# Statistics in smaller pieces between two additions, and two blocks that stay in fast memory, in a four-layer scan kernel

## The chip, the cores and the metric

The kernel runs on one core of a Trainium2 chip. The metric is device time in microseconds (us) of one execution. Several executions of the same kernel are run, and their median is given. One further execution is taken by the hardware profiler; all profile views come from that one. Engines are named as in the profile: PE (TensorE matmul), PEld (its weight load), DVE (VectorE), ACT (ScalarE), POOL (GpSimd), SP (SyncE, which issues DMAs).

## The reference

The input is 4 x 48 x 256 x 256 numbers in float32. Four layers follow each other, each of the form x + layer(group norm of x). Layers 0 and 1 are an attention over channels and a gated convolution; the change does not touch them. Layers 2 and 3 are scans in four directions, with a five-tap convolution at each step:

```python
def step(w, b):
    def f(carry, inp):
        nxt = inp + _conv1d(carry, w, b)
        return (nxt, nxt)
    return f
# down over rows, up over rows (same weights), right over columns, left over columns
x = x + _L2_conv_ref(_gn(x), ...)   # scans' layer 0 below
x = x + _L3_conv_ref(_gn(x), ...)   # scans' layer 1 below
```

The group norm ahead of layer 3 needs mean and variance of the result of layer 2, over groups of three channels and all pixels.

## The kernel before

The four images are worked on as two pairs of two. For each pair the function `chain` writes one chain of steps: in each of two layers 256 steps down, 256 up, 256 right, 256 left. Of the two layers, `layer == 0` is the reference's layer 2 and `layer == 1` its layer 3. In a step (line 1067 and the lines after it) each image of the pair, `b`, has three matmuls into a PSUM bank `ps`, and then one addition on DVE that makes the new `carry` from `ps` and the step's input (line 1071 or 1075). The next step of the same image starts from this `carry`. The two images of a pair alternate, so that PE multiplies for one while DVE adds for the other.

The first pair's chain starts some 990 steps ahead of the second's (`LEAD`). So the first pair does nearly all of its first layer alone, then both chains share the engines step by step, and the second pair does nearly all of its last layer alone. The instructions of an engine run in one order that the framework's scheduler fixes when the kernel is built, from the order of writing and from priorities; `keep_in_program_order` holds an instruction in its written place. `look` (line 1044) is a tiny addition on DVE that reads one number of a buffer written three steps earlier; it is held in this way.

Columns are treated in NK = 16 blocks of CB = 16 steps. A buffer, called a slot, holds one block of one pair: 96 partitions x 4096 numbers, 1536 KB. Each pair has a ring of five slots, and `slot(name)` or `take(pair, name)` gives the next. In the right scan `lines` collects a block's results with an addition of the bias on ACT (line 1291), and at the end of the block it is stored in DRAM as `R` (line 1305). `pre` are columns copied on POOL (line 1264). The left scan goes through the blocks backwards. At the first step of block n it issues, on SP, the load of `lines` of block n - 1 from `R` (line 1327) and that of `stage`, the layer's input to which the result is added (line 1328). For each step POOL adds the new carry to a column of `stage` (line 1339), and at the end of the block `stage` is stored (line 1359). In the last layer of the second pair (`direct`) POOL writes instead into two buffers `done` (line 1343), taken from the first pair's ring, one for each image and holding two blocks; they are stored straight into the output by `write` (line 1371). By then the first pair is finished; its slots were last used by `to_rows`, which brings the first pair's result into rows with copies on POOL and ACT (lines 1450 and 1452) while the second pair runs its last layer. The list `times` says at which steps its pieces are written.

In `layer == 0` the left scan also takes the statistics for the next group norm. For each block, `late` gets 8 pieces: for each image four times `bn_stats` over 512 numbers (line 1380). One is taken out at the end of each of the following steps. After the last block the remaining ones are written, then for each image one `bn_aggr` over all 64 pieces, which gives `mv` (line 1400), then the group norm's two short pieces, each with a matmul (lines 88 to 99).

Of the kernel before, what the change touches and what calls it, by code (L numbers as in the profile page):

```python
# [9 lines left out]
F32 = mybir.dt.float32  # L10
# [8 lines left out]
NP = 2  # L19
P = 96  # L20
# [5 lines left out]
NK = W // (2 * KC)  # L26
# [938 lines left out]
def scans(ctx, tc, xs, out, wts, biases, dram, k, coefs, lead, spare):  # L965
# [13 lines left out]
    nc = tc.nc  # L979
# [42 lines left out]
    def chain(pair):  # L1022
# [23 lines left out]
        def slot(name):  # L1046
            return take(pair, f"{name}{pair}")
# [55 lines left out]
        def layer_of(layer, first):  # L1103
# [33 lines left out]
            for n in range(NT):  # L1137
                ahead_ = None
                for r in range(RT):
# [12 lines left out]
                    def keep(new, b):  # L1152
                        nc.scalar.activation(inp[:, b], blocks(new[:, b]), AF.Identity, bias=bias[:, 0:1])  # L1153
# [111 lines left out]
                fetched[g] = t  # L1265

            kept.clear()
            column = columns[0]
            for w in range(1, far):
                fetch(column, 0, w)  # L1270
            for n in range(NK):
                ahead_ = None
                for w in range(CB):
                    if w == 0 and n == 0:
                        ahead_ = columns[1]
                    elif w == 0 and n + 1 < NK:
                        ahead_ = slot("col")
                        nc.sync.dma_start(by_batch(ahead_), block_of(U, n + 1))
                    if w == 0 and n + 1 == NK:
                        stage = slot("stage")  # L1280
                        nc.sync.dma_start(by_batch(stage), block_of(x, n))
                    if w == 0:
                        lines = slot("lines")
                    if w + far < CB:
                        fetch(column, n, w + far)
                    elif ahead_ is not None:
                        fetch(ahead_, n + 1, w + far - CB)
                    line = lines_view(lines)[:, w]

                    def keep(new, b):  # L1290
                        nc.scalar.activation(line[:, b], new[:, b], AF.Identity, bias=bias[:, 2:3])  # L1291

                    if n == 0 and w == 0:

                        nc.vector.tensor_scalar(  # L1295
                            advance(), cols_view(column)[:, :, 0, :, 0], bias[:, 1:2], None, ALU.subtract
                        )
                        keep(inner(), slice(0, 2))
                    else:
                        step(layer, 1, fetched.pop(n * CB + w), keep)  # L1300
                    if n + 1 < NK or w + 1 < CB:
                        look(line[:, 1, 0:1], fetched[n * CB + w + 1][:, 1, 0:1])
                    yield
                if ahead_ is not None:
                    nc.sync.dma_start(Rt[n], lines)
                    column = ahead_


            late = []
            if layer == 0:  # L1310
                stats = [wp.tile([P, NK * 4, 6], F32, tag=f"st{pair}{b}", name="st") for b in range(2)]
            following = None
            kept.clear()

# [5 lines left out]
            for n in reversed(range(NK)):  # L1320
# [2 lines left out]
                    done = [take(0, "done") for _ in range(2)]  # L1323
                for w in reversed(range(CB)):
                    if w == CB - 1 and n > 0:
                        ahead_ = slot("lines"), slot("stage")
                        nc.sync.dma_start(ahead_[0], Rt[n - 1])
                        nc.sync.dma_start(by_batch(ahead_[1]), block_of(x, n - 1))
                    if layer == 0 and n == 0 and w == CB // 2:
                        following = [slot("dn"), slot("dn")]  # L1330
                        for r in range(2):
                            load_rows(1, 0, r, following[r], 1, NK)
                    line = lines_view(lines)[:, w]
                    to = cols_view(stage)[:, :, w % 2, :, w // 2]

                    def keep(new, b):
                        if not direct:
                            if b.stop == 2:
                                nc.gpsimd.tensor_add(to, to, new)  # L1339
                            return  # L1340
                        for i in range(b.start, b.stop):
                            place = done[i].rearrange("p (h w) -> p h w", w=2 * CB)[:, :, n % 2 * CB + w]
                            nc.gpsimd.tensor_add(place, to[:, i], new[:, i])  # L1343

                    if n == NK - 1 and w == CB - 1:
                        keep(inner(), slice(0, 2))
                    else:
                        step(layer, 2, line, keep)
                    if direct:
                        look(done[1].rearrange("p (h w) -> p h w", w=2 * CB)[:, 0, n % 2 * CB + w : n % 2 * CB + w + 1])  # L1350
                    else:
                        look(to[:, 1, 0:1])
                    if late:
                        late.pop(0)()
                    if writes and w % 8 == 4:
                        writes.pop(0)()
                    yield
# [19 lines left out]
                if layer == 0:  # L1377

                    def stat(b, c, n=n, v=by_batch(stage)):
                        nc.vector.bn_stats(stats[b][:, n * 4 + c, :], v[:, b, c * 512 : (c + 1) * 512])  # L1380

                    late += [lambda b=b, c=c, f=stat: f(b, c) for b in range(2) for c in range(4)]
                    if n == 0:
                        for r in range(2):
                            for q in range(2):
                                nc.sync.dma_start(
                                    rows_view(following[r])[q * C : (q + 1) * C, :, 0].rearrange("c b h w -> c b (h w)"),
                                    cols_view(stage)[r * C : (r + 1) * C, :, q, :NH, :].rearrange("c b h w -> c b (h w)"),
                                )
# [4 lines left out]
            if layer == 0:  # L1394

                ends = []
                for b in range(2):
                    mv = work.tile([P, 2], F32, tag=f"mv{pair}{b}", name="mv")
                    late.append(
                        lambda b=b, mv=mv: nc.vector.bn_aggr(mv, stats[b].rearrange("p a b -> p (a b)"))  # L1400
                    )
                    ends.append(k.group_norm_pieces(work, p_small, mv, "mean6", coefs[3][2 * pair + b], f"{pair}{b}"))
                for piece in late:
                    piece()
                    yield
                for i in range(2):
                    for both in ends:
                        both[i]()
                    yield
                yield following  # L1410
# [58 lines left out]

    engines = [nc.gpsimd] * 4  # L1470
    pieces = to_rows(0, engines)
    times = [20 + 26 * i for i in range(16)] + [530 + 24 * i for i in range(8)]
    for i, _ in enumerate(chains[1]):
        if i == times[16]:
            engines[3] = nc.scalar
# [127 lines left out]
```

## Time and profile before

| what | value |
|---|---|
| median of 3 runs | 8981.94 us (8981.17 to 8982.99) |
| the profiled execution | 8983.88 us; its span 8982.1 us |
| mean granted clock of PE | 0.983 |
| PE busy | 8646.3 us, 96% of the span |
| DVE busy | 4167.5 us, 46% |
| ACT busy | 3479.8 us, 39% |
| POOL busy | 1948.9 us, 22% |
| matmuls of the scans (line 1067) | 48960 records, 5423.7 us busy, 12 for each step of a pair |
| statistics of the left scan (line 1380) | 256, 172.3 us busy |
| aggregates after the left scan (line 1400) | 4, 7.4 us busy |

A line of the group view reads: line, engine, operation, tiles out<-in, shapes, count | busy time and mean ns of one | idle time of the engine before them, and what ended it. A line of the windows view reads: window, its length, busy time (and instructions) of PE, PEld, DVE, ACT and POOL, then the mean granted clock of PE, the mean busy share of the 16 DMA engines, and GB/s. A line of the timeline reads: start, length, engine, source line, operation, tiles, shapes, count, and in brackets the engine's idle time and what ended it. In the chain of waits the first column is the start and the second the length of a piece, and each piece released the next. Times count from the start of the span.

In the profiled execution the first statistic of the first pair begins at 4537.0 us, the last one of the second pair at 7495.2 us. The second pair's last left scan has its first addition at 8594.7 and the last at 8949.2 us.

### The profile page before, as it was taken

The page shows a single profiled execution, that of the slowest core. Times are in us where ns is not written, and L with a number is a line of the kernel's source. Part 1 is how long each engine was busy: PE and PEld are TensorE (multiplying, and loading weights), DVE is VectorE, ACT ScalarE, POOL GpSimd, SP SyncE. Part 2 cuts the span into 40 slices and gives each one's busy share as a digit, 9 for nine tenths or more (in the row PEclk, how much of TensorE's full clock was granted, in tenths as well). Part 3 has the DMA queues.
Part 4 walks back from the last instruction along what each step waited for, and adds up shares of the span by engine and source line. Part 5 has one row for each costly group of instructions (what it writes and reads, how often), then busy time and mean ns, then how long its engine had stood idle before and what let it go on. Part 6 is the DMA issues. An engine that isn't in the chain of part 4 may idle for free. (4 is left out here: it accounts for less than half of the span.)

```text
span 8982.1 us, 162711 instructions
## 1 busy us (share of the span) xinstructions
PE 8646.3 (96%) x62920; PEld 7223.1 (80%) x62920; DVE 4167.5 (46%) x15625; ACT 3479.8 (39%) x7023; POOL 1948.9 (22%) x3100
## 2 busy tenths in 40 slices
PE   6999999999999978999999999999999999999998
PEld 4777777533333335999999999999999999999998
DVE  3231110234555555445666444445666555444653
ACT  0010101123433455766601776666663003665610
POOL 0000000001111111001454000001445664101575
PEclk9999999999999988999999999999999999999998
DMA  7654323367888876765577664556656887867789
GB/s 152 132 125 94 74 61 77 82 140 160 173 181 182 182 165 162 168 138 143 155 190 190 152 139 120 141 135 141 169 146 175 216 220 181 198 172 191 210 176 183
DMA packets 1180233, 1390.64 MB, mean 155 GB/s; under 512 B 263184, under 2 KB 1107216, under 8 KB 1118784
## 3 DMA queue, kind: packets, MB, share of 16 engines
q1 hardware_dynamic: 1179360, 1379.90, 65.7%
q8 instruction: 493, 8.08, 0.4%
q14 instruction: 284, 2.33, 0.1%
q0 software_dynamic: 96, 0.33, 0.0%
HBM read 811.21 MB, written 509.61 MB: 147 GB/s over the span
## 5 line engine op out<-in xcount | busy, mean ns | idle before, releaser
L1067 PE MATMUL ps<-carry,w 96*96 96x128 f32 x48960 | 5423.7, 273 | 59.3 <-DVE carry L1071 29.1
L1067 PEld LDWEIGHTS ps<-carry,w 96*96 96x96 f32 x48960 | 5397.6, 163 | 95.0 <-issue 44.9
L1264 POOL COPY pre<-col 96x256 f32<-96x256 f32 x1020 | 657.5, 646 | 2682.2 <-DMA col<-last 1964.1
L1153 ACT ACTIVATE dn<-carry,b 96x128 f32<-96x128 f32 (+1 forms) x2044 | 769.0, 398 | 796.8 <-DVE carry L1071 789.0
L1291 ACT ACTIVATE lines<-carry,b 96x128 f32<-96x128 f32 (+1 forms) x2044 | 819.8, 402 | 583.9 <-DVE carry L1075 574.0
L1071 DVE TENSOR_TENSOR carry<-ps,dn 96x128 f32<-96x128 f32 x2280 | 653.2, 288 | 806.1 <-PE ps L1067 781.2
L1199 ACT ACTIVATE up<-carry,b 96x128 f32<-96x128 f32 x1792 | 719.5, 402 | 459.9 <-DVE carry L1071 459.6
L1075 DVE TENSOR_TENSOR carry<-ps,lines 96x128 f32<-96x128 f32 x2040 | 576.8, 286 | 562.8 <-PE ps L1067 552.9
L1075 DVE TENSOR_TENSOR carry<-ps,pre 96x128 f32<-96x128 f32 x2040 | 586.7, 288 | 457.6 <-PE ps L1067 402.4
L1071 DVE TENSOR_TENSOR carry<-ps,up 96x128 f32<-96x128 f32 x1792 | 516.0, 288 | 598.1 <-PE ps L1067 592.8
L1339 POOL TENSOR_TENSOR stage<-stage,carry 96x256 f32<-96x256 f32 x768 | 657.4, 857 | 470.4 <-DVE seen L1044 436.7
L581 PE MATMUL py<-x1n,wy 128*96 128x512 f32 x1536 | 703.1, 607 | 30.9 <-ACT x1n L541 28.4
L295 PE MATMUL acc<-xs,xt 128*96 128x288 f32 x2048 | 667.2, 408 | 0.0
L294 PE MATMUL acc<-xt 128*96 128x288 f32 x2048 | 666.8, 409 | 0.0
L581 PEld LDWEIGHTS py<-x1n,wy 128*96 128x96 f32 x1536 | 244.2, 165 | 454.7 <-issue 437.1
L279 DVE COPY xt<-pt 128x384 f32<-128x384 f32 x256 | 136.7, 555 | 849.0 <-PE pt L276 645.8
L261 ACT ACTIVATE xn<-raw,coef 96x2048 f32<-96x2048 f32 x64 | 133.7, 2095 | 987.0 <-PE pt L276 819.6
L296 PE MATMUL acc<-xt,xs 128*96 128x192 f32 x2048 | 502.1, 327 | 0.0
L296 PEld LDWEIGHTS acc<-xt,xs 128*96 128x96 f32 x2048 | 332.4, 165 | 154.5 <-issue 1.8
L295 PEld LDWEIGHTS acc<-xs,xt 128*96 128x96 f32 x2048 | 332.2, 165 | 151.4 <-issue 2.8
L604 DVE TENSOR_TENSOR y<-py,t 96x512 f32<-96x512 f32 x256 | 171.4, 678 | 593.3 <-PE py L590 584.4
L590 PE MATMUL py<-x2n,wy 64*96 64x512 f32 x1536 | 363.0, 601 | 0.0
(186 smaller groups left out, 5542.7 us busy)
## 6 DMA issues: line engine op xcount, KB each, us to landing
stage<-x SPq DMA_DIRECT2D x64, 1536.0 KB
dn<-x SPq DMA_DIRECT2D x240, 384.0 KB
R<-lines SPq DMA_DIRECT2D x60, 1536.0 KB
lines<-R SPq DMA_DIRECT2D x60, 1536.0 KB
D<-dn SPq DMA_DIRECT2D x56, 1536.0 KB
up<-D SPq DMA_DIRECT2D x56, 1536.0 KB
U<-up SPq DMA_DIRECT2D x224, 384.0 KB
col<-U SPq DMA_DIRECT2D x56, 1536.0 KB
```

The source lines that it names most:

```text
L294: nc.tensor.matmul(acc[0], lhsT=xt[:, h + 2, :], rhs=xt[:, here, :], start=first, stop=last)
L295: nc.tensor.matmul(acc[1], lhsT=xt[:, h + 2, :], rhs=xs[:, here, :], start=first, stop=last)
L296: nc.tensor.matmul(acc[2], lhsT=xs[:, h + 2, :], rhs=xt[:, past, :], start=first, stop=last)
L581: nc.tensor.matmul(ps, lhsT=held["w"][0][:, dx], rhs=x1n[:, 2 * c : 2 * c + 2, dx : dx + W], start=dx == 0, stop=False)
L1067: nc.tensor.matmul(ps, lhsT=w_sb[layer][:, way, j, :], rhs=old[:, i, j : j + W // 2], start=j == 0, stop=j == 2)
L1071: nc.vector.tensor_add(new[:, i].rearrange("p (k w) -> p k w", w=KC), ps.rearrange("p (k w) -> p k w", w=KC), inp[:, i])
L1075: nc.vector.tensor_add(new[:, i], ps, inp[:, i])
L1153: nc.scalar.activation(inp[:, b], blocks(new[:, b]), AF.Identity, bias=bias[:, 0:1])
L1199: nc.scalar.activation(place[:, b], blocks(new[:, b]), AF.Identity, bias=bias[:, 1:2])
L1264: nc.gpsimd.tensor_copy(t, cols_view(block)[:, :, w % 2, :, w // 2])
L1291: nc.scalar.activation(line[:, b], new[:, b], AF.Identity, bias=bias[:, 2:3])
L1339: nc.gpsimd.tensor_add(to, to, new)
```

## The change

The statistics are taken in pieces of 256 numbers, 16 for each block, one in each step of the next block. Each is placed between the step's two additions: `keep` is called after an addition, and takes a piece out of `late` where it is called for the first image. Each of them is held in its written place. After eight pieces an image's block is aggregated into `means`. At the end of the layer, `total` makes `mv` from the 16 blocks' means and variances: the mean of the means, and the mean of the variances plus the variance of the means. The remaining pieces are written two to a step.

In the second pair's last layer, the right scan's blocks NK - 3 and NK - 2 go into two slots of the first pair's ring (`staying`). They are neither stored in `R` nor loaded from it. The last eight of the `times` of `to_rows` are moved from 530 + 24 i to 526 + 22 i, so that its last piece is written before these two slots are taken.

```diff
             kept.clear()
+            staying = {}
             column = columns[0]
@@ right scan, first step of a block
-                        lines = slot("lines")
+                        if n in (NK - 3, NK - 2) and layer == 1 and pair == NP - 1:
+                            if not staying:
+                                staying.update((i, take(0, "lines")) for i in (NK - 2, NK - 3))
+                            lines = staying[n]
+                        else:
+                            lines = slot("lines")
@@ right scan, end of a block
-                    nc.sync.dma_start(Rt[n], lines)
+                    if n not in staying:
+                        nc.sync.dma_start(Rt[n], lines)
@@ left scan
-                stats = [wp.tile([P, NK * 4, 6], F32, tag=f"st{pair}{b}", name="st") for b in range(2)]
+                stats = [wp.tile([P, 8, 6], F32, tag=f"part{pair}{b}", name="part") for b in range(2)]
+                means = [wp.tile([P, NK, 2], F32, tag=f"means{pair}{b}", name="means") for b in range(2)]
...
-                        ahead_ = slot("lines"), slot("stage")
-                        nc.sync.dma_start(ahead_[0], Rt[n - 1])
+                        ahead_ = staying.get(n - 1) or slot("lines"), slot("stage")
+                        if n - 1 not in staying:
+                            nc.sync.dma_start(ahead_[0], Rt[n - 1])
...
                     def keep(new, b):
+                        if b.start == 0 and late:
+                            late.pop(0)()
...
-                    if late:
-                        late.pop(0)()
...
                     def stat(b, c, n=n, v=by_batch(stage)):
-                        nc.vector.bn_stats(stats[b][:, n * 4 + c, :], v[:, b, c * 512 : (c + 1) * 512])
-
-                    late += [lambda b=b, c=c, f=stat: f(b, c) for b in range(2) for c in range(4)]
+                        tc.keep_in_program_order(nc.vector.bn_stats(stats[b][:, c, :], v[:, b, c * 256 : (c + 1) * 256]))
+                        if c == 7:
+                            nc.vector.bn_aggr(means[b][:, n, :], stats[b].rearrange("p a b -> p (a b)"))
+
+                    late += [lambda b=b, c=c, f=stat: f(b, c) for b in range(2) for c in range(8)]
...
-                    late.append(
-                        lambda b=b, mv=mv: nc.vector.bn_aggr(mv, stats[b].rearrange("p a b -> p (a b)"))
-                    )
+                    def total(b=b, mv=mv):
+                        both = work.tile([P, 2, 2], F32, tag=f"both{pair}{b}", name="both")
+                        for i in range(2):
+                            nc.vector.bn_stats(stats[b][:, i, :], means[b][:, :, 1 - i])
+                            nc.vector.bn_aggr(both[:, i, :], stats[b][:, i, :])
+                        nc.vector.tensor_copy(mv[:, 0:1], both[:, 1, 0:1])
+                        nc.vector.tensor_add(mv[:, 1:2], both[:, 0, 0:1], both[:, 1, 1:2])
+                    late.append(total)
...
-                for piece in late:
-                    piece()
+                for i in range(0, len(late), 2):
+                    for piece in late[i : i + 2]:
+                        piece()
                     yield
@@ end of scans
-    times = [20 + 26 * i for i in range(16)] + [530 + 24 * i for i in range(8)]
+    times = [20 + 26 * i for i in range(16)] + [526 + 22 * i for i in range(8)]
```

## The prediction

> **What bounds the kernel now.** I read the chain of waits first, then windows, groups and timelines of the stages that it points at.
>
> ```profile
> PE 46%; DVE 1%; DMA 1%; POOL 0%; issue 0%; ACT 0%; SPq 0%; POOLq 0%; DVEq 0%; ACTq 0%
> PE ps L1067 46%; DMA stage<-x 1%; DVE st L1380 0%; POOL stage L1339 0%; DVE carry L1075 0%; DMA lines<-R 0%; ACT dn L1125 0%; DVE seen L1044 0%; POOL done L1343 0%; DVE carry L1071 0%; SPq L1213 0%; DVE mv L1400 0%; DMA col<-last 0%; DVE carry L1295 0%; ACT carry L1130 0%
> ```
>
> The scans are a chain of matmuls. The change can remove none of them, only the gaps in it. A step has two halves, one for each batch, each with one addition on DVE. In undisturbed work one addition follows another every 0.656 us (below, 4570.45 to 4571.11), set by PE. So the loss of any stretch is its length minus additions times 0.656. Three stretches that the change touches have losses.
>
> **Stretch A, the first pair's left scan of its first layer**, which has TensorE nearly to itself:
>
> ```profile
> L1075 DVE TENSOR_TENSOR carry<-ps,lines 96x128 f32<-96x128 f32 x452 | 126.5, 285 | 103.3 <-PE ps L1067 102.2
> L1380 DVE BATCH_NORM_STATS2 st<-stage 96x6 f32<-96x512 f32 x114 | 75.5, 681 | 17.8 <-POOL stage L1339 17.8
> L1071 DVE TENSOR_TENSOR carry<-ps,dn 96x128 f32<-96x128 f32 x28 | 6.6, 278 | 0.0
> ```
>
> These are groups of 4536 to 4870 us: 452 + 28 = 480 additions are worth 314.9 us, the stretch has 334, so 19.1 are lost, some 1.35 in each of 14 blocks. The timeline of DVE shows how:
>
> ```profile
> 4563.64 1.27 DVE L1380 BATCH_NORM_STATS2 st<-stage 96x6 f32<-96x512 f32 x2
> 4564.83 0.56 DVE L1075 TENSOR_TENSOR carry<-ps,lines 96x128 f32<-96x128 f32 x2
> 4565.31 0.14 DVE L1044 TENSOR_TENSOR seen<-zero,stage 96x1 f32<-96x1 f32 x1
> 4565.38 1.27 DVE L1380 BATCH_NORM_STATS2 st<-stage 96x6 f32<-96x512 f32 x2
> ...
> 4570.45 0.29 DVE L1075 TENSOR_TENSOR carry<-ps,lines 96x128 f32<-96x128 f32 x1 [0.30 <-PE ps L1067]
> 4571.11 0.29 DVE L1075 TENSOR_TENSOR carry<-ps,lines 96x128 f32<-96x128 f32 x1 [0.37 <-PE ps L1067]
> 4571.32 0.14 DVE L1044 TENSOR_TENSOR seen<-zero,stage 96x1 f32<-96x1 f32 x1
> ```
>
> Two statistics stand between two steps and hold both additions: such a step takes 1.74 us instead of 1.31. Further down DVE is idle 0.30 to 0.37 us before each addition.
>
> **Stretch B, the two seams** after each pair's first layer, and **stretch C, the last left scan**, in windows:
>
> ```profile
> 4914.00:4925.00 11.00, 9.02 (x54) 8.80 (x54) 5.73 (x21) 3.51 (x9) 0.00 (x0) 0.69 1.11 229
> 7496.00:7508.00 12.00, 9.71 (x56) 9.28 (x55) 7.31 (x20) 0.00 (x0) 3.57 (x5) 0.72 0.84 261
> 8600.00:8640.00 40.00, 40.00 (x368) 40.00 (x367) 19.62 (x91) 0.00 (x0) 31.69 (x62) 1.00 0.47 103
> 8640.00:8940.00 300.00, 289.60 (x2553) 288.14 (x2552) 136.92 (x639) 0.00 (x0) 215.12 (x426) 0.97 1.09 198
> ```
>
> The last three columns are granted clock, DMA share and GB/s. At the seams the clock falls: two aggregates (L1400, 1.87 us each) stop the additions. Counting as above, 4904 to 4935 has 37 additions (24.3 of 31 us, 6.7 lost) and 7487 to 7530 has 52 (34.1 of 43, 8.9 lost). In the last scan DMA is half idle until 8640, then full to the end. Its chain of waits:
>
> ```profile
> 8845.03 16.35 DMA stage<-x
> ...
> 8892.94 16.91 DMA stage<-x
> ...
> 8911.44 37.61 PE ps L1067 x318
> ```
>
> Two blocks take 47.9 us, 24.0 each, while PE needs 16 x 1.312 = 21.0. From 8594.7 to 8949.2 the 510 additions are worth 334.6 of 354.5 us: 20 lost.
>
> [...] and the one-element look takes 0.145. [...] after the second aggregate four additions come 1.28 us apart, and the clock reads 0.69 and 0.72. [...] the result stores here are 128-byte packets, and their stage is the one that DMA bounds.
>
> **The change part by part.**
>
> *Halved statistics, in A.* 16 a block instead of 8. [...] the next operation starts some 80 ns before the end (pairs above: 1.27 for two), so 0.33 us of DVE. In the built order each stands between the first and second addition of a step. First addition at 0, the statistic from 0.21 (add to look above), DVE free at 0.54, second addition due at 0.656: it fits with 0.11 to spare, so steps cost nothing; PE hides them. Once a block the first statistic waits for POOL's last addition (857 ns, started just after the look): it begins about 1.0 us after the previous step's second addition ends, and holds the next second addition to 1.33 instead of 1.02. Of these 0.31 us some 0.2 is slack in the loop (0.656 less 0.29 for the addition and about 0.15 of hand-over). I take 0.15 a block, 2 us. The partial aggregates, twice a block, have 48 numbers instead of 384: [...] behind the second addition, in a gap of 0.37 plus the slack: nothing. A: 19.1 - 2 - 0.6 for what the stretch loses anyway, **16.5 us gained**; ends 19 and, if half the fit fails, 9.
>
> *What is queued behind.* A block's buffer is now held until its last statistic, at the end of the next block, so the lines load that takes this buffer is issued some 10 us later: in the trace mid-block (4551.30), now at the boundary. SP is in order; behind it stand the store of x (waits for POOL) and then the stage load, which changes places with the store. By the windows around these issues the lines load is 6.2 us of DMA time, store and stage 10.8: 17.0 in all, started within 3 us of the boundary and needed 21 later. It fits with about 1 us to spare; cost nothing, bound 1 us a block. The second pair's left scan shares PE with the other chain and has 42 us a block; the additions there come at PE's pace both before and, with the same margins, after: nothing.
>
> *Totals, in B.* The two aggregates (3.7 us) go. In their place for each batch come a 0.36 aggregate, two small statistics, two tiny aggregates, a copy and an addition, at 0.15 to 0.2 us each: 1.3 for each batch, 2.6 in all, and the built order scatters them among additions. Left-over statistics go two a step (0.66 us in a 0.37 gap, about 0.1 lost on each of 8 steps). One wait of PE for mv stays (0.9 in the trace); I expect no half clock. Left 3 to 3.5 us a seam: 3.7 and 5.4, **9 us gained**; ends 2 and 13.
>
> *Two blocks kept, in C.* Removed: two stores and two loads of 1536 KB; the loads stood at 8581 and 8590, in the half-idle part, so their 13 us are not themselves on the path. What moves is what follows: their buffers take stage 13, lines 12 and lines 11 a block earlier. Per block DMA then needs 5.4 (stage), 6.5 (lines), 12 (two stores), 24 in all. I lay these in order of issue from 8635, where the stores begin. Before: four transfers on each boundary from the start, queue empty at 8707 after the third batch. After: 8701, with some 6 us idle before it because no buffer is free. Thereafter both run at 24 a block, so the end moves by **6 us**; ends 0 (another order of stores eats it) and 14 (no idle). The earlier times of the regrouping (526 + 22 i) change nothing: its last copies end at 8472 already, before the kept blocks begin at about 8532.
>
> **Sum.** 16.5 + 9 + 6 = 31.5. The profiled execution took 8983.9 (span 8982.1), 1.9 over the median 8981.9; so 8952.4 by its own time, **8950** by the median. What a measurement of this kernel can tell from no change is about 0.2%, 18 us.
>
> **Rivals.** *Only the left statistics pay*: C is bound by DMA throughout, the loads removed lay in idle time, and the seams keep their waits for mv. 8982 - 16.5 = 8965. *The fit is short*: each step late by z; 14 blocks of 16 steps are 224 z; at z = 0.075 A gains nothing and 8967 is left. For it: the margin is 0.11 by estimate. Against: the spare slack of 0.2 behind it. *Slower*: the late lines load of A. If store, stage and lines together need 21 + y us from the boundary, each block loses y and A gains nothing; 14 y > 15 + 18 needs y = 2.4, which means 23.4 us where 17.0 are measured plus a start of 3. At y = 4 it would be 9023. Against it: the measured share of 0.74. *That the change does not do what it says*: the built order shows every statistic where it should be and the two loads gone.
>
> **Chances.** The forecast 0.60 (8938 to 8962), only the left statistics 0.16, the short fit 0.14, slower 0.07, undecided 0.03. Split at 8964 and 9000 this gives faster 0.79, same 0.13, slower 0.08. Range 8934 to 8974: it takes in the ends of the parts, not all at once, and the first two rivals.
>
> **What would show it.** In A one statistic between two additions 0.656 apart, about 0.41 us long, and no pair of them; the stretch 17 us shorter. At the seams no aggregate over 0.4 us and a clock near 1. In C DMA busier before 8640, the first stage wait two or three blocks later. I am wrong if additions in A come slower than 0.66, if lines or stage waits appear there, or if the last left still has seven blocks of 24 us.

## Result, and the profile after

The changed kernel took 8936.19 us, the median of 8932.44, 8934.35, 8938.04 and 8942.68; the kernel before took 8981.56 beside it. The ratio is 0.9955 (95% interval 0.9943 to 0.9968): faster by 45 us, half a per cent, where 31.5 had been forecast. 8936.19 lies inside the stated range of 8934 to 8974, but near its end, and 2 us outside the narrower 8938 to 8962 that the forecast itself was given. A second set on another occasion gave 8940.83 against 8975.04, ratio 0.9958 (0.9946 to 0.9971), which is 34 us. The median of all nine runs of the changed kernel is 8938.0. The kernel before had medians from 8974.5 to 8977.2 in later sets of 8 to 36 runs. So the difference is about 38 us, and the first comparison flattered it.

The profiled execution spans 8932.6 us (run: 8934.35). Its chain of waits has the same share of PE, and the statistics have all but left it:

```profile
PE 46%; DMA 1%; issue 0%; POOL 0%; DVE 0%; ACT 0%; SPq 0%; POOLq 0%; DVEq 0%; ACTq 0%
PE ps L1067 46%; DMA stage<-x 1%; DMA oi<-result 0%; DMA lines<-R 0%; POOL stage L1352 0%; ACT dn L1125 0%; POOL done L1356 0%; DVE carry L1071 0%; DVE carry L1075 0%; SPq L1213 0%; DVE part L1391 0%; DVE seen L1044 0%; ACT up L1199 0%; DVE carry L1302 0%; DMA col<-last 0%
```

**Stretch A after.** The groups of DVE from 4523 to 4841 us, which are the same 480 additions; after the shapes each line gives busy time and mean ns, then the idle time ahead of them and its releaser:

```profile
L1075 DVE TENSOR_TENSOR carry<-ps,lines 96x128 f32<-96x128 f32 x454 | 130.6, 288 | 70.7 <-PE ps L1067 60.8
L1391 DVE BATCH_NORM_STATS2 part<-stage 96x6 f32<-96x256 f32 x225 | 92.9, 413 | 4.4 <-POOL stage L1352 4.4
L1393 DVE BATCH_NORM_AGGREGATE means<-part 96x2 f32<-96x48 f32 x28 | 10.0, 356 | 0.0
L1071 DVE TENSOR_TENSOR carry<-ps,dn 96x128 f32<-96x128 f32 x26 | 7.5, 289 | 7.8 <-PE ps L1067 7.5
```

DVE does more here than before (92.9 + 10.0 us of statistics and aggregates against 75.5), yet 480 additions fit in 318 us instead of 334. The timeline of DVE at the start of a block's statistics shows why:

```profile
4568.22 0.29 DVE L1075 TENSOR_TENSOR carry<-ps,lines 96x128 f32<-96x128 f32 x1
4568.82 0.42 DVE L1391 BATCH_NORM_STATS2 part<-stage 96x6 f32<-96x256 f32 x1 [0.31 <-POOL stage L1352]
4569.17 0.27 DVE L1075 TENSOR_TENSOR carry<-ps,lines 96x128 f32<-96x128 f32 x1
...
4571.08 0.29 DVE L1075 TENSOR_TENSOR carry<-ps,lines 96x128 f32<-96x128 f32 x1 [0.30 <-PE ps L1067]
4571.29 0.41 DVE L1391 BATCH_NORM_STATS2 part<-stage 96x6 f32<-96x256 f32 x1
4571.74 0.29 DVE L1075 TENSOR_TENSOR carry<-ps,lines 96x128 f32<-96x128 f32 x1
4571.94 0.14 DVE L1044 TENSOR_TENSOR seen<-zero,stage 96x1 f32<-96x1 f32 x1
4572.39 0.29 DVE L1075 TENSOR_TENSOR carry<-ps,lines 96x128 f32<-96x128 f32 x1 [0.30 <-PE ps L1067]
```

From 4571.08 on additions stand 0.66 and 0.65 apart, though a statistic lies between the first two: it costs nothing. The first one of a block waits for POOL, and its addition comes 0.95 us after the last instead of 0.656. Over a whole block 0.24 us are lost, where the kernel before lost 1.35.

**Stretches B and C after**, in windows (in the last three columns clock, DMA share and GB/s). The first two take in the group norm's matmuls, which stand at 4891.1 and 4892.6 and at 7469.5 and 7471.2 us:

```profile
4872.00:4903.00 31.00, 31.00 (x279) 30.30 (x278) 22.74 (x113) 18.92 (x44) 2.56 (x3) 1.00 1.03 239
7452.00:7495.00 43.00, 42.85 (x383) 41.67 (x382) 29.10 (x142) 18.32 (x25) 20.59 (x24) 1.00 1.02 217
8560.00:8600.00 40.00, 40.00 (x368) 40.00 (x367) 19.57 (x93) 0.00 (x0) 31.66 (x62) 1.00 0.41 89
8600.00:8900.00 300.00, 291.80 (x2610) 290.50 (x2609) 139.21 (x652) 0.00 (x0) 220.68 (x436) 0.98 1.05 191
```

At both seams PE is busy nearly throughout, at full clock, and no longer waits for `mv`. In the last left scan DMA is still full for 300 us. The chain of waits of that scan names its first long DMA wait 216 us after the scan's first addition at 8555.3 (before: 8772.80, 178 us after 8594.7):

```profile
8559.99 207.40 PE ps L1067 x1895
...
8771.17 15.98 DMA lines<-R
...
8800.27 9.82 DMA stage<-x
...
8823.75 15.18 DMA stage<-x
...
8847.15 8.95 DMA stage<-x
...
8872.15 15.71 DMA stage<-x
```

Counting the additions from the start of the scan, the kernel before does nine blocks at PE's 21.0 us and the changed one ten; most of the rest take 22 to 27 us in both. In all traces of the study it is eight or nine without kept blocks, and ten or eleven with them.

**Where the time went, place by place.** In every trace I count the additions that read `ps` (8160, both pairs) and take how long a run of them lasts, less its length in the first trace of before. This table holds all kernels of the study; a negative number is a gain, in us. "Start" is up to addition 0, "A" 1600 to 2080, "seam 1" 2080 to 2160, "seam 2" 6000 to 6090, "down" 6300 to 6800 (the down scan of the second pair's last layer), "C" 7600 to the last, "drain" from the last addition to the end of the span.

| kernel | start | A | seam 1 | seam 2 | down | C | drain |
|---|---|---|---|---|---|---|---|
| before, second trace | +0.1 | -0.1 | +0.2 | 0.0 | +0.1 | -2.7 | -0.2 |
| after | -9.2 | -15.5 | -5.6 | -6.2 | +0.6 | -6.1 | -3.9 |
| after, second trace | -12.9 | -15.5 | -5.6 | -6.2 | -1.8 | -6.4 | -3.9 |
| stats_only | -1.8 | -15.5 | -5.6 | -6.2 | +0.5 | +2.2 | +0.4 |
| totals_only | -1.3 | +1.2 | -4.9 | -5.6 | -1.1 | 0.0 | -0.1 |
| keep_only | +3.0 | 0.0 | +0.3 | +0.1 | 0.0 | -5.7 | -3.6 |
| nopin | -6.2 | -9.1 | -5.0 | -5.3 | -2.4 | -4.6 | -5.8 |
| s512_pinned | -2.3 | -8.4 | -4.5 | -4.8 | -1.3 | -6.5 | -3.6 |
| rows_spaced | -8.5 | -15.6 | -5.6 | -6.2 | -2.2 | -5.6 | -4.2 |
| ring_turned | -5.3 | -0.1 | +0.2 | 0.0 | 0.0 | +2.2 | -3.2 |
| norm_pin | +3.7 | -15.5 | -5.6 | -6.2 | -1.8 | -6.7 | -3.7 |
| norm_pin2 | -3.7 | -15.5 | +5.4 | -6.2 | -17.3 | -3.7 | -3.8 |
| norm_pin_last | -5.3 | -15.5 | -5.6 | -6.2 | -17.3 | -5.9 | -3.6 |

The changed places sum to 15.5 + 5.6 + 6.2 + 6.1 + 3.9 = 37.3 us, which matches the 38 of the pooled medians. The "start" column, in layers that the change does not touch, is most of what the first comparison had on top. Additions 0 to 1600, which the table leaves out, move by -4.4 to +0.5 us; there the first trace of before was some 4 us slower than most others.

### The profile page after: what moved, and what is told of

It reads as the page before. It is cut to its first block, busy times and chain, and to the rows that moved or that the text cites. A ratio compares the mean times of both kernels' runs of the same rounds, so it can differ in the third digit from the quotient of the medians.

```text
span 8932.6 us, 162995 instructions
## 1 busy us (share of the span) xinstructions
PE 8617.9 (96%) x62920; PEld 7206.7 (81%) x62920; DVE 4215.2 (47%) x15965; ACT 3480.3 (39%) x7023; POOL 1945.7 (22%) x3100
## 5 line engine op out<-in xcount | busy, mean ns | idle before, releaser
L581 PE MATMUL py<-x1n,wy 128*96 128x512 f32 x1536 | 698.7, 604 | 31.5 <-ACT x1n L541 28.4
```

Of the source, the lines that this page charges most:

```text
L581: nc.tensor.matmul(ps, lhsT=held["w"][0][:, dx], rhs=x1n[:, 2 * c : 2 * c + 2, dx : dx + W], start=dx == 0, stop=False)
```

## The experiments

My theory was that the change works in three independent places: gaps of DVE in A, long aggregates at the seams, and the DMA queue of the last left scan. The rivals were that only part of it pays, that the size or the place of the statistic alone decides, and that the 9 to 13 us of the early layers belong to the change.

### stats_only: the change without the kept blocks

```
-                        if n in (NK - 3, NK - 2) and layer == 1 and pair == NP - 1:
-                            ...
-                            lines = staying[n]
-                        else:
-                            lines = slot("lines")
+                        lines = slot("lines")
...
-    times = [20 + 26 * i for i in range(16)] + [526 + 22 * i for i in range(8)]
+    times = [20 + 26 * i for i in range(16)] + [530 + 24 * i for i in range(8)]
```

> The change without its kept blocks and with the old times of the regrouping: new statistics and new totals alone. My theory (gaps on the vector engine): the first pair's left scan of its first layer gains 15 to 16 us, the two seams 5 to 6 each, the last left scan nothing (still blocks of 24 us from about 8700), so 27 us in the changed places. The two traces so far differ by another 12 us in layers that no edit touches. If that is chance of a single run, this kernel's median lies at 8950 to 8958 and its early layers may look like either trace; if it comes with the new statistics (another layout of the memory, say), the median is 8942 and its trace has additions 560 to 1600 some 12 us ahead of before's. Rival (the seams pay by the smaller clock loss only, the scan nothing): 8970.

Measured: 8950.97 us against 8975.04, ratio 0.9974 (0.9964 to 0.9985). A and both seams gain to 0.1 us what the whole change gains there; the last left scan gains nothing. The three gains sum to 27.3; less the 2.6 us that its last scan and drain lost, 24.7 are left, and the medians differ by 24.1. So in eight runs with the new statistics nothing is left over for the early layers.

### totals_only: statistics of 512 in their old place, only the aggregation new

```
-                        tc.keep_in_program_order(nc.vector.bn_stats(stats[b][:, c, :], v[:, b, c * 256 : (c + 1) * 256]))
-                        if c == 7:
+                        nc.vector.bn_stats(stats[b][:, c, :], v[:, b, c * 512 : (c + 1) * 512])
+                        if c == 3:
```

and `late` is popped after `look` again, with four pieces for an image (`range(4)`), nothing kept and the old times.

> Statistics of 512 numbers in their old place at the end of a step, as before, but aggregated block by block, with the short total at the seam; nothing kept, old times. My theory: the seams gain as in the change, 5.6 and 6.2 us, with no half clock there; the left scan keeps its loss of some 19 us, or 1 to 3 us more, since two small aggregates a block (0.36 us) join the pairs of statistics. Median 8970, range 8966 to 8973. Rival (the half clock at the seam comes from PE's wait for the group norm, not from the long aggregates): the clock there stays at 0.7 and the gain is under 5 us, 8977.

Measured: 8966.35, ratio 0.9990 (0.9982 to 0.9998). A loses 1.2 us more than before, and the seams gain 4.9 and 5.6. Here are two lines of PE's timeline in the kernel before, at its first seam, and then windows of totals_only at the two seams, with the clock third from the right. The windows take in its group norm's matmuls, at 4913.4 and 7498.0 us:

```profile
4914.90 0.33 PE L88 MATMUL pg<-mv,cst 96*96 96x1 f32 x2 [0.90 <-DVE mv L1400]
4917.05 7.14 PE L1067 MATMUL ps<-carry,w 96*96 96x128 f32 x36 [1.08 <-DVE gn_m L89]
```

```profile
4904.00:4935.00 31.00, 30.17 (x271) 29.49 (x270) 19.63 (x92) 21.84 (x49) 0.86 (x1) 1.00 0.98 215
7465.00:7508.00 43.00, 41.86 (x377) 40.92 (x376) 26.74 (x127) 6.92 (x7) 24.99 (x30) 1.00 0.80 182
```

The clock is 1.00, with the same group norm behind the totals. So the half clock of the kernel before, 0.50 from 4916.4 to 4923 and from 7500.3 to 7507, came with the long aggregates. Before, PE waited 0.90 us for `mv`, the result of such an aggregate; here it waits for additions alone, 0.6 us at most. The run takes away both effects of the aggregate, the held additions and PE's wait for `mv`, and does not tell them apart.

### keep_only: the two kept blocks and the new times alone

The lines of the change that concern `staying` and `times`, on the kernel before.

> The kernel before with the two kept blocks and the new times of the regrouping, statistics and totals as before. My theory: nothing moves up to the last left scan; that gains 6 us because the loads of the blocks after the kept ones are issued a batch earlier, into the half-idle DMA time: median 8975 to 8976, the DMA share before the first two thirds of the first 40 us of that scan higher than 0.47. Rival (the removed loads lay in idle time, so nothing): 8981.5. Second rival (the whole 12 us of the two loads come off): 8969. If the 12 us of the early layers came with the kept blocks or the times, the median would be 8963.

Measured: 8963.67 against 8975.04, ratio 0.9987 (0.9981 to 0.9994), 11 us where 6 were expected. The trace has 5.7 in the scan and 3.6 in the drain. The expected DMA share was wrong too; the windows of keep_only:

```profile
8600.00:8640.00 40.00, 40.00 (x368) 40.00 (x367) 19.69 (x92) 0.00 (x0) 31.74 (x62) 1.00 0.43 92
8640.00:8940.00 300.00, 290.37 (x2606) 289.08 (x2605) 139.17 (x651) 0.00 (x0) 221.69 (x435) 0.98 1.05 190
```

DMA is not busier in the first 40 us (0.43, before 0.47). This kernel does eleven blocks at 21.0 us.

### after_again and before_again: second traces

No edit.

> The changed kernel once more, for a second trace and more runs. Theory of chance: in its early layers (before 3250 us) this trace shows another pattern of half-clock windows than the first one, its median lies between 8934 and 8946, and the stretches that the change touches give the same 15.5, 5.6, 6.2 and 6 us within 1 us. Rival (the early 12 us belong to the change): the same early windows as in its first trace, 8936 within 3 us.

> The kernel before once more, for a second trace. Theory of chance: its early layers show other half-clock windows than its first trace, up to 12 us earlier or equal, and its runs spread over 8970 to 8984. Rival (the early 12 us belong to the change): additions 560 to 1600 within 2 us of the first trace's, and all runs within 8979 to 8984.

Measured: 8940.83 (8927.22 to 8943.14) and 8974.53 (8962.93 to 8987.79, 13 runs). The changed places repeat within 0.3 us, C of before within 2.7. Taken alone these two speak for the rival: each second trace nearly repeats its own kernel's early part (+0.1, and -12.9 after -9.2). More traces are needed. Windows from 440 to 530 us of before, before_again, after_again and norm_pin, in this order; that is the first layers' work:

```profile
440.00:530.00 90.00, 87.69 (x479) 66.71 (x478) 28.34 (x75) 12.92 (x10) 3.95 (x16) 0.91 0.51 110
```

```profile
440.00:530.00 90.00, 87.69 (x495) 66.58 (x494) 28.33 (x75) 12.91 (x10) 3.94 (x16) 0.94 0.52 111
```

```profile
440.00:530.00 90.00, 87.69 (x516) 67.50 (x515) 28.05 (x75) 12.91 (x10) 3.95 (x16) 1.00 0.53 111
```

```profile
440.00:530.00 90.00, 87.69 (x501) 67.00 (x500) 28.21 (x76) 12.91 (x10) 3.96 (x16) 0.96 0.53 111
```

PE is busy 87.69 us in each, yet it does 479 to 516 matmuls, as the granted clock goes from 0.91 to 1.00. norm_pin carries the new statistics and has lost clock here; ring_turned, with the old ones, has none below 1. But in this window the clock is 1.00 in six of the eight traces with statistics of 256 and in one of the six with 512, so the traces alone do not settle it. The medians of many runs say more: for the change, stats_only, totals_only and keep_only they differ from before by 38, 24, 9 and 11 us, and the changed places sum to 37, 25, 9 and 9. That leaves little for the early layers, and I take their 9 to 13 us to be largely chance. The mean of "start" is -1.0 us over the six traces with statistics of 512 and -5.5 over the eight with 256, with spreads of 8 and 17 us; a few us that do belong to the new statistics are not excluded.

### nopin: the same place in the program, not pinned

```
-                        tc.keep_in_program_order(nc.vector.bn_stats(stats[b][:, c, :], v[:, b, c * 256 : (c + 1) * 256]))
+                        nc.vector.bn_stats(stats[b][:, c, :], v[:, b, c * 256 : (c + 1) * 256])
```

> The change with its statistics written at the same place but not pinned there, so that the scheduler places them. In its list it puts two statistics between the additions of a step and a third after the second addition, and other matmuls move as well. My theory (a gap holds one statistic of 0.33 us of the vector engine, not two): each such step comes late by 0.25 to 0.35 us, some five or six steps a block, so 1.5 to 2 us a block of 21 against 0.3 in the change; the left scan loses its whole gain, some 15 to 25 us, median 8952 to 8962. Rival (the size alone pays, the place does not matter): 8936 as the change.

Measured: 8940.88, ratio 0.9961 (0.9949 to 0.9974); A gains 9.1 instead of 15.5. Both sides missed: the place matters, by 6.4 us, and not by 15 to 25. Timeline of DVE in nopin:

```profile
4572.70 0.42 DVE L1391 BATCH_NORM_STATS2 part<-stage 96x6 f32<-96x256 f32 x1 [0.90 <-POOL stage L1352]
4573.05 0.27 DVE L1075 TENSOR_TENSOR carry<-ps,lines 96x128 f32<-96x128 f32 x1
4573.24 0.41 DVE L1391 BATCH_NORM_STATS2 part<-stage 96x6 f32<-96x256 f32 x1
4573.57 0.27 DVE L1075 TENSOR_TENSOR carry<-ps,lines 96x128 f32<-96x128 f32 x1
4573.76 0.14 DVE L1044 TENSOR_TENSOR seen<-zero,stage 96x1 f32<-96x1 f32 x1
4573.82 0.74 DVE L1391 BATCH_NORM_STATS2 part<-stage 96x6 f32<-96x256 f32 x2
4574.48 0.27 DVE L1075 TENSOR_TENSOR carry<-ps,lines 96x128 f32<-96x128 f32 x1
```

Two statistics take 0.74 in one gap, and the next addition comes at 0.91. But one wait for POOL (0.90) and a rush of statistics behind it cost a block 0.33 or 1.11 us in turn, since part of it is caught up in the rest of the block. How much of the 6.4 us belongs to the bunching and how much to the longer wait for POOL (0.90 instead of 0.31) is not shown apart.

### s512_pinned: the place without the size

Statistics of 512 numbers, one in each of 8 steps, pinned between the additions (`c * 512`, `if c == 3`, `range(4)` in the change).

> The change with statistics of 512 numbers, one each step pinned between the two additions, 8 a block. My theory: the statistic stands from 0.21 to about 0.81 us after the first addition and the second is due at 0.656, so it comes 0.15 late; the changed kernel's trace shows that nearly all of such a delay stays (0.28 late, 0.24 lost), so 0.11 to 0.15 in each of 8 steps, 0.9 to 1.2 a block, 13 to 17 us over the 14 blocks: the scan gains 0 to 5 us instead of 15.5, median 8946 to 8952. Rival (the place pays and the loop has 0.2 us of slack, as my prediction took): nothing lost, 8936.

Measured: 8947.34, ratio 0.9966 (0.9954 to 0.9979). The median lies where the theory had it, but A gains 8.4, between the two theories. The timeline of DVE in s512_pinned, statistics and additions of three steps and the aggregate between them:

```profile
4578.15 0.29 DVE L1075 TENSOR_TENSOR carry<-ps,lines 96x128 f32<-96x128 f32 x1 [0.30 <-PE ps L1067]
4578.36 0.68 DVE L1391 BATCH_NORM_STATS2 part<-stage 96x6 f32<-96x512 f32 x1
4578.96 0.27 DVE L1075 TENSOR_TENSOR carry<-ps,lines 96x128 f32<-96x128 f32 x1
...
4579.47 0.29 DVE L1075 TENSOR_TENSOR carry<-ps,lines 96x128 f32<-96x128 f32 x1 [0.17 <-PE ps L1067]
4579.67 0.68 DVE L1391 BATCH_NORM_STATS2 part<-stage 96x6 f32<-96x512 f32 x1
4580.27 0.27 DVE L1075 TENSOR_TENSOR carry<-ps,lines 96x128 f32<-96x128 f32 x1
4580.46 0.25 DVE L1393 BATCH_NORM_AGGREGATE means<-part 96x2 f32<-96x24 f32 x1
...
4580.88 0.29 DVE L1075 TENSOR_TENSOR carry<-ps,lines 96x128 f32<-96x128 f32 x1
```

The second addition comes 0.81 after the first, 0.15 late as expected, but the next step begins 1.32 after the last: this delay is absorbed. The step after that takes 1.41. So a block loses 0.3 over six or seven such steps, and 0.5 at its first statistic, which waits for POOL and then holds DVE 0.6: 0.80 in all. So the loop has slack, but less than the 0.2 us that the prediction took: two delays of 0.15 cost 0.10 together, and in the changed kernel 0.29 at a block's first statistic cost 0.24. The place alone is worth 8.4 us in A and the size alone, in nopin, 9.1; together they give 15.5, so the two overlap.

### rows_spaced: other times for the regrouping

The changed kernel still loses some 17 us between 7640 and 7800.

```
-    times = [20 + 26 * i for i in range(16)] + [526 + 22 * i for i in range(8)]
+    times = [21 + 32 * i for i in range(7)] + [240 + 24 * i for i in range(8)] + [520 + 20 * i for i in range(9)]
```

> The change with other times for the first pair's regrouping during the second pair's last layer: 7 pieces 32 steps apart in the down scan, each some 10 steps ahead of a block's boundary (behind the boundary's own loads), 8 pieces 24 apart in the up scan, 9 pieces 20 apart in the right scan. The changed kernel loses 17 to 18 us between 7640 and 7800 where the norm of a down block waits for loads that share DMA with the regrouping's. My theory: with its transfers behind those loads 10 to 17 us of that go, and the denser right scan costs up to 3: median 8922 to 8930. Rival (the D stores and down loads are late by themselves, or POOL's copies hold the right scan): no gain or a loss, 8934 to 8945.

Measured: 8936.20, ratio 0.9959 (0.9946 to 0.9971), the same as the changed kernel. The theory fell, and the trace shows it sharply, since PE's gaps there have the same lengths to 0.01 us although the transfers moved. The timeline of DVE in the changed kernel, and one line of ACT's, show what does hold it:

```profile
7646.65 0.29 DVE L1071 TENSOR_TENSOR carry<-ps,dn 96x128 f32<-96x128 f32 x1 [0.42 <-ACT dn L1153]
7647.99 0.29 DVE L1071 TENSOR_TENSOR carry<-ps,dn 96x128 f32<-96x128 f32 x1 [1.06 <-PE ps L1067]
7650.73 0.29 DVE L1071 TENSOR_TENSOR carry<-ps,dn 96x128 f32<-96x128 f32 x1 [2.45 <-ACT dn L1125]
7652.73 0.29 DVE L1071 TENSOR_TENSOR carry<-ps,dn 96x128 f32<-96x128 f32 x1 [1.71 <-PE ps L1067]
7654.01 0.29 DVE L1071 TENSOR_TENSOR carry<-ps,dn 96x128 f32<-96x128 f32 x1 [0.99 <-PE ps L1067]
7655.29 0.29 DVE L1071 TENSOR_TENSOR carry<-ps,dn 96x128 f32<-96x128 f32 x1 [0.99 <-PE ps L1067]
```

```profile
7648.62 2.08 ACT L1125 ACTIVATE dn<-dn,biased 96x2048 f32<-96x2048 f32 x1
```

A norm of 2.08 us (L1125) stands on ACT right ahead of the addition that reads it. After that gap the additions come 1.28 us apart, twice 0.656 less a little: the half clock again, 0.50 from 7651.2 to 7658. A gap of PE of 3.28 us, up to 7651.17, stands right ahead of it. The clock is 0.50 once more from 7784.4 to 7794.4; there the gap ahead is 1.87 us, up to 7784.42, and one of 3.21 follows. At the first seam before, above, the gaps were 0.90 and 1.08 us. How long a gap brings the half clock is not shown.

### norm_pin, norm_pin2, norm_pin_last: the norms earlier

```
-                nc.scalar.activation(v, v, AF.Identity, bias=g[:, 1:2], scale=g[:, 0:1])
+                pin(nc.scalar.activation(v, v, AF.Identity, bias=g[:, 1:2], scale=g[:, 0:1]))
...
-                        nc.scalar.activation(inp[:, b], blocks(new[:, b]), AF.Identity, bias=bias[:, 0:1])
+                        pin(nc.scalar.activation(inp[:, b], blocks(new[:, b]), AF.Identity, bias=bias[:, 0:1]))
```

`pin` is `tc.keep_in_program_order`: in norm_pin for the first line alone, in norm_pin2 for both, in norm_pin_last for both in the second pair's last layer only.

> The change with the down scans' norms (the 2 us operations of the scalar engine that prepare the next block) pinned in program order. The trace after the respaced regrouping shows the same gaps of PE to 0.01 us as without it (3.28, 1.28, 1.87 and 3.21 between 7640 and 7800), so they do not come from DMA: two norms stand right before the additions that read them, the vector engine waits 2.45 us for one, and the half clock follows. My theory: pinned, they stand earlier at least in part of the blocks; the stretch from addition 6300 to 6800 gains 5 to 16 us. Rival (a pinned norm waits for its block's load and holds up the scalar engine in the scans where both chains run): losses elsewhere eat it, 8936 or more.

> As the last, with the scalar engine's own writes of the down rows pinned too, so that every norm stands where the program has it: 11, 14, 22 and 25 rows into the block. My theory: the stretch from addition 6300 to 6800 loses nearly nothing and gains 15 to 17 us, median 8920 to 8924. Rival: the norm at row 22 comes 29 us into the block and the load that it reads is issued about 10 us in and takes some 25, so the scalar engine waits there up to 6 us in each block: no gain.

> The change with norms and down writes pinned in the second pair's last layer alone. Pinned everywhere they gained 17.3 us in that layer, and lost 11 at the first seam (5.4 us slower than before instead of 5.6 faster) and 2 to 3 at the start of the scans. My theory: the places are independent, so this kernel keeps the 17 us (additions 6300 to 6800) and has the change's -15.5, -5.6 and -6.2 in the other places; about 17 us under the change, median 8918 to 8925, ratio to the kernel before 0.9940 or less. Rival (the loss at the seam was a load order that moves with any pinning): the seam loses again, 8930 or more.

Measured: 8936.83, 8933.00 and 8930.56 us; ratios 0.9956 (0.9944 to 0.9969), 0.9950 (0.9938 to 0.9962) and 0.9947 (0.9933 to 0.9961). Pinning the norms alone changes nothing, against the 5 to 16 us expected of it. With the writes pinned too the down scan gains 17.3 us, but everywhere it turns the first seam from -5.6 to +5.4. In the last layer alone it keeps both. The windows from 7640 to 7820, first of norm_pin_last, then of the changed kernel, with busy PE first:

```profile
7640.00:7820.00 180.00, 180.00 (x1643) 179.90 (x1642) 86.90 (x398) 135.60 (x292) 15.04 (x14) 1.00 0.83 197
```

```profile
7640.00:7820.00 180.00, 169.62 (x1482) 168.53 (x1481) 78.29 (x358) 124.26 (x264) 12.97 (x12) 0.95 0.84 194
```

PE has no gap left at the same DMA share, so the order on ACT held the down scan, and not the loads. norm_pin_last has the lowest median of the study, 7.5 us under the pooled median of the changed kernel. That misses the expected 17, though the trace has 17.3 in the down scan; its interval overlaps with that of the changed kernel, so a gain in whole runs is not shown. What pinning does at the first seam was not followed further.

### ring_turned: other buffers for the last result

```
             direct = layer == 1 and pair == NP - 1
+            for _ in range(2 if direct else 0):
+                buffers[0].pools.append(buffers[0].pools.pop(0))
```

> The kernel before, with the ring of the first pair's buffers turned by two places ahead of the last left scan, as the two kept blocks turn it, and nothing else. The kept blocks gained 9.3 to 10.3 us where I had laid out 6: the additions came 6 earlier, and the last stores ended 28.4 to 28.8 us after the last addition instead of 32.2 to 32.8. Theory of place (other buffers hold the last result blocks, whose stores then run faster): this kernel's stores end 28 to 29 us after the last addition too, and it gains 3 to 4 us in all. Theory of the queue (fewer transfers are left in the queue at the last addition): 32 to 33 us as before, no gain.

Measured: 8977.93, ratio 1.0000 (0.9991 to 1.0008), no gain in all, though one of 3 us could not be seen in this interval. But the drain is 29.2 us, 3.2 shorter, with all transfers of before in place. So the turned ring by itself gives the shorter drain, and no transfer need be dropped for it. The last four stores were issued 0.3, 2.5, 8.6 and 13.0 us after the last addition, as with kept blocks, against 0.3, 5.6, 13.4 and 18.9 before.

Why it is shorter is not shown. Some 29000 packets were left at the last addition, as in the change, against 31000 before. That is about 2 us less work at before's pace, so a shorter queue is part of it; the rest went a little faster (1061 packets a us against 1020). Nor is it shown that the end comes sooner for it: the scan lost 2.2 us here, within its spread, so the end came 1.0 us sooner than in the first trace of before and later than in the second.

## Why the prediction was right, step by step

- **A, 16.5 forecast, 15.5 measured.** Statistic 0.41 estimated, 0.413 measured. The estimate can be worked out from two rows of before, L1380 with 681 ns for 512 numbers and L1044 with 145 ns for one: 145 + 255 x (681 - 145)/511 = 412 ns. So two small ones are 0.83 us of busy DVE where one of 512 was 0.68, and yet A gained, by the gaps that they lie in. Aggregate 0.36 estimated, 0.356 measured; the same 145 ns, with the 1874 ns that L1400 took for 384 numbers, gives 145 + 47 x (1874 - 145)/383 = 357 ns. What was mis-sized is the cost of the wait for POOL at a block's first statistic: 0.15 us a block taken, 0.24 lost. The delay itself was right (0.31 forecast, 0.29 measured); the slack of 0.2 us behind it was not, since only 0.05 was made up. No lines or stage wait appeared; the late lines load cost nothing, so the slower rival falls.
- **The short fit** falls for 256 numbers. s512_pinned shows where it begins: with 0.15 us of overrun about 0.05 is lost for each statistic, and the loop's slack takes the rest.
- **B, 3.7 and 5.4 forecast, 5.6 and 6.2 measured.** The step "left 3 to 3.5 us a seam" was too careful: 1.1 and 2.7 are left (6.7 - 5.6 and 8.9 - 6.2), or 2.1 and 2.3 counted over the additions of the table. One term of it failed: "one wait of PE for mv stays (0.9)". In the changed kernel's trace PE does not wait for `mv` at either seam. The half clock went, as said: 1.00 in both windows. What had set it off is not shown; PE's gaps there, before, were 0.90 and 1.08 us at the first seam and 0.72 and 1.56 us at the second. totals_only shows that the aggregates are most of it (4.9 and 5.6), and the smaller, pinned statistics the last 0.6 to 0.7.
- **C, 6 forecast; 6.1 to the last addition, 10.0 to the end.** The shift of the additions was right, within a spread of some 5 us among kernels that keep no block. The step that failed is the end: I took the last addition's gain for the span's. Behind it the drain was another 3.9 us shorter. ring_turned gives a drain as short by the turn of the ring alone, which the prediction left out: it laid out transfers by order and size and never by the buffer. That the whole 3.9 comes from there is not shown, since ring_turned itself ends between the two traces of before. Also wrong was the sign at "DMA busier before 8640": 0.41 instead of 0.47. The loads did move forward as laid out: counted from the scan's first addition, the stage load of block 13 is issued at -25.9 us instead of 19.4, and the lines loads of blocks 12 and 11 at -4.9 and 20.0 instead of 20.1 and 47.7. But what moved to before the scan's start is missing from these 40 us, and the first stage load among the stores stands behind two of them, at 49.1, where before it stood behind one, at 41.0. The first DMA wait of the chain came 38 us later, just under two blocks, at the near end of the two or three forecast; by the lengths of the blocks it is one more at PE's pace, and two in keep_only.
- **Only the left statistics pay** falls: the seams give 11.8 and the end 10.
- **Sum.** 31.5 forecast against 37.3 in the places: -1.0 in A, +2.7 at the seams, +0.1 and +3.9 in C. So the parts were right in kind, and A and the additions of C in size; the sum is 6 us short, through the seams and the drain. The rest of the first comparison's 45 us lay mostly in the early layers, where the two traces differ in half-clock windows; a few us of it are open, as said above. The first median still fell inside the range by 2 us, and that of all nine runs by 4. The drain, which the prediction did not see, took up most of the room at that end, so that the range held is in part luck.

## What to carry to other kernels

When a small operation runs beside a tight chain, ask which gap it lies in and how long that is, not what it costs in all: here 27 us more of DVE work made the stretch 15.5 us shorter. A gap that holds one statistic of 0.33 us did not hold two (0.74 us in nopin, the next addition 0.91 after the last), and with a scheduler that is free to bunch them 6 of those 15.5 us were lost again. Compare two kernels by how long the same stretch of work takes in each trace; gains of 6 us at the seams repeat to 0.1 there (the last scan, bound by DMA, only to some 3), while whole runs of one kernel differ by 20.

## What was not expected

- The stores of 128-byte packets were done 3.2 to 5.8 us sooner after the last addition when the ring had been turned (26.6 to 29.2 us against 32.2 to 32.8). Whether the place of the buffers does it, or which transfers had been done by then, is open.
- The granted clock in the first layers falls to half (0.50), mostly for 3.4 to 13.7 us and once in each trace for 24 to 41 us, at places of which some change between runs: 95 to 130 us of such windows in the first 3240 us. In the first trace of before, those at 500, 913 and 1308 us begin although PE has no gap over 0.25 us in the 14 us ahead of them, so idle time of PE does not explain these; what does is open.
- Norms of 2.08 us on ACT, late by less than 3 us each, cost some 6 and 9 us in two stretches of 20 us (7640 and 7780): PE had gaps of 3.28, 1.87 and 3.21 us there, and the granted clock stood at 0.50 for 6.8 and 10 us.
